# Bias of the values added to the tokens on GpSimd, values evicted as copies, statistics aggregated in groups, and a handicap for VectorE in the planner

## The chip, the cores and the metric

The kernel runs on one core of a Trainium2 chip. The metric is the device time of one execution in microseconds (us). A core has five engines with instruction queues of their own: TensorE (PE in the profile, with PEld for its weight loads), VectorE (DVE), ScalarE (ACT), GpSimd (POOL) and SyncE (SP), which issues most transfers. Each engine works through its queue in the order in which it was written; semaphores hold an instruction back until what it reads is there.

## The reference

Four sequences of 1024 tokens with 256 features go through attention, a channel mix, a state-space block and the channel mix again, each on a normalized copy and added to the token stream `x`:

```python
x = x + _L0_attn_a_ref(_layernorm(x, axis=-1), Wq, bq, Wk, bk, Wv, bv)
x = x + _L0_ffn_ref(_layernorm(x, axis=-1), W_r, W_k, W_v, mu_r, mu_k)
x = x + _L0_attn_b_ref(_layernorm(x, axis=-1), ...)   # state-space block
x = x + _L0_ffn_ref(_layernorm(x, axis=-1), W_r, W_k, W_v, mu_r, mu_k)
```

What the change touches is the attention and the layer norm:

```python
V = jnp.einsum('nsd,ed->nse', X, Wv) + bv
scores = jnp.einsum('nqd,nkd->nqk', Q, K) / scale
scores = jnp.where(causal, -jnp.inf, scores)
weights = jax.nn.softmax(scores, axis=-1)
return jnp.einsum('nqk,nkd->nqd', weights, V)

m = jnp.mean(x, axis=axis, keepdims=True)
v = jnp.var(x, axis=axis, keepdims=True)
return (x - m) / jnp.sqrt(v + eps)
```

The rows of `weights` sum to 1, so `weights @ (V0 + bv)` equals `weights @ V0 + bv`: the bias of the values may be added to `V`, or to what attention adds to.

## The kernel before

**Tiles.** `x[b]` holds the tokens of sequence b on the chip: 128 partitions, 8 row tiles of 256 features. A half `j` (0 to 7) is four row tiles, half a sequence. A row tile `i` runs from 0 to 31. Letters name the stage: `a` attention, `f` the first channel mix, `h` the state-space block, `g` the second channel mix.

**Layer norm.** `normalized` serves all four stages. For each of the four row tiles of a half, `stats(n)` issues bn_stats (L622) and bn_aggr (L623) on VectorE, one behind the other. `ve` adds the epsilon on VectorE (L648, L650), `rs` raises to the power -1/2 on GpSimd (L661), `mrs` makes the shift on VectorE (L670), and `xn` scales and shifts each row tile on VectorE (L676) or ScalarE (L682). In stage g, halves 0 to 5 take their statistics from sums on ScalarE instead. The normalized rows are then turned: through a tile in DRAM and a VectorE transpose (L750), or by TensorE.

**Attention.** `queries` folds the query and key weights into one product. `values(i)` (L1522) multiplies a row tile with `wv`, which has 257 columns: the last is a term that the keys' bias adds to a key's score. VectorE evicts the product into `v` and adds `bv_r` in one instruction (L1532); the 257th column of `bv_r` belongs to that term. `scores(i)` makes the scores (L1550) in a pair of PSUM banks; `least` on VectorE adds the mask (L1560) and, with the 257th column of `v`, takes the least element (L1566); ScalarE exponentiates (L1571). `turn_by_dram` turns the exponentials through DRAM (transpose L1608), `weigh(i)` multiplies them with `v` (L1655), and `a.x` scales and adds that to `x` on VectorE (L1664).

**The rest.** `stream_sums` (T, L832), the gating product `y` (L1965) and `keys_of_batch` feed `seven_products`, which makes four 128x128 block products with seven multiplications (`held_...`, L858); copies between its steps (L783 ScalarE, L784 VectorE) stand on its chain. The channel mixes add to `x` on GpSimd (L1101), the state-space block adds its output bias there too (L1699).

**The planner.** No order is written out by hand. `Order` collects operations with what they need, one or more ways (engine, cost in us, what to emit), and the PSUM bank that they free; matrix products are units. It works out due times backwards and then runs a simulation forwards: at each step `_way` takes the way of an operation that ends first, `_first` the operation with the earliest due time among those that can start about now. `DVE+port` marks VectorE instructions that it doesn't lay beside GpSimd work. Units come from a window of 9, the one that can start soonest. It tries 20 settings with 5 rounds each, keeps the one that ends first by its own clock, and emits the queues in that order. So a changed cost can change the order of every engine in every stage. `PSUM` has 4 single banks and 2 pairs. In the loop over `i`, scores are laid two or three row tiles ahead of `weigh`, values one more.

The lines that the steps below turn on:

```python
        return min(
            (self._start(time, w) + w[1], self._start(time, w), w[0], w[2])
            for w in self.log[n]["ways"]
        )
```

Of the kernel before, what the change touches and what calls it, by code (L numbers as in the profile page):

```python
# [19 lines left out]
P = 128  # L20
NB = 4
L = 1024
D = 256
# [4 lines left out]
NH = NT // 2  # L28
KC = D // P
HALF = 512  # L30
# [23 lines left out]
class Order:  # L54
# [15 lines left out]
    FLIGHT, LANDING = 1.2, 0.24  # L70
    HOLD = 30.0
    SURE = 0.5
    FRONT = 12.0


# [180 lines left out]
    def _way(self, time, n):  # L256

        if self.log[n]["moves"]:
            time = max(time, self.queue - self.FLIGHT - 0.5)
        return min(  # L260
            (self._start(time, w) + w[1], self._start(time, w), w[0], w[2])
            for w in self.log[n]["ways"]
        )

    def _start(self, time, way):
        engine, _, port = way[0].partition("+")
# [93 lines left out]
def dve(n):  # L360
    return 0.02 + n / 850
# [7 lines left out]
def hybrid_kernel(  # L369
# [34 lines left out]
    nc = tc.nc  # L404
# [179 lines left out]
    def normalized(  # L584
# [35 lines left out]

        def stats(n):
            nc.vector.bn_stats(st()[:, n, :], row(n))  # L622
            nc.vector.bn_aggr(mv()[:, n, :], st()[:, n, :])  # L623

        def sums(n):
            nc.scalar.activation(
# [66 lines left out]
        if by_scalar:  # L693
            for n in range(NH):
                o.op(f"{key}.su{n}", [needs[n]], ("ACT", act(D) + 0.11, partial(sums, n)))
            o.op(f"{key}.me", [f"{key}.su{n}" for n in range(NH)], ("POOL", 0.2, means))
            for n in range(NH):
                o.op(f"{key}.st{n}", [f"{key}.me"], ("ACT", act(D) + 0.11, partial(squares, n)))
            variances_of = lambda n0, n1: by_sums()
            shifts_of = lambda n0, n1: shifts_by_sums()  # L700
        else:
            for n in range(NH):
                o.op(f"{key}.st{n}", [needs[n]], ("DVE", 0.53, partial(stats, n)))
            variances_of, shifts_of = variances, shifts
        for n0, n1 in spans:
            span = "" if n1 - n0 == NH else f"{n0}"
            some = range(n0, n1)
            o.op(
                f"{key}.ve{span}", [f"{key}.st{n}" for n in some],
                ("DVE+port", 0.08 * k, partial(variances_of, n0, n1)),  # L710
            )
            o.op(
                f"{key}.rs{span}", [f"{key}.ve{span}"],
                ("POOL", 0.4 + 0.62 * k, partial(powers, n0, n1)),
            )
            o.op(
                f"{key}.mrs{span}", [f"{key}.rs{span}"],
                ("DVE+port", 0.08 * k, partial(shifts_of, n0, n1)),
            )
            for n in some:  # L720
                o.op(
                    f"{key}.xn{n}", [f"{key}.mrs{span}"],
                    ("DVE+port", dve(D), partial(on_vector_by_sums if by_scalar else on_vector, n)),
                    ("ACT", act(D) + 0.1, partial(on_scalar, n)),
                )
# [89 lines left out]
    def stream_sums(key, src, needs):  # L815

        t = [lazy(lambda k=k: cols(f"T{k}_{key}")) for k in range(KC)]

        def b(c, h):
            return src(h)[:, c, :]  # L820

        def sums(k):
            return t[(k - 1) // 2]()[:, (k - 1) % 2, :]

        for k, plus, minus in (
            (1, lambda: b(0, 1), lambda: b(0, 0)),
            (3, lambda: b(1, 1), lambda: b(0, 1)),
            (2, lambda: b(1, 1), lambda: sums(1)),
            (4, lambda: b(1, 0), lambda: sums(2)),
        ):  # L830
            def emit(engine, k=k, plus=plus, minus=minus):
                engine.tensor_sub(sums(k), plus(), minus())  # L832

            o.op(
                f"{key}.T{k}", needs + ([f"{key}.T{k - 1}"] if k in (2, 4) else []),
                ("POOL", 1.05, partial(emit, nc.gpsimd)), ("DVE+port", dve(HALF), partial(emit, nc.vector)),
            )
        return sums

# [597 lines left out]
    def attend_prepare(j, by_hand=False):  # L1437
# [5 lines left out]
            spans=((0, 2), (2, NH)) if j == 0 else ((0, NH),), by_scalar=False,  # L1443
        )

    def attend_transpose(j, spans=((0, NH),)):

        xn, needs, _, _ = xa_rows.pop(j)
# [63 lines left out]
    def values(i):  # L1512
# [7 lines left out]
        def emit():  # L1520
# [8 lines left out]
        )  # L1529
        o.op(  # L1530
            f"v{i}", [f"pv{i}"],
            ("DVE", dve(D), lambda: nc.vector.tensor_add(t()[:, n, :], pv()[:, : D + 1], bv_r)),  # L1532
            frees="bank",
        )

    def scores(i):
# [43 lines left out]
            + ["constants"],  # L1580
            emit, "pair",
        )
        o.op(f"p{i}", [f"sc{i}", f"v{i}"], ("DVE", dve(nk) + 0.3, least), frees="pair")
        o.op(f"e{i}", [f"p{i}"], ("ACT", act(nk) + 0.11, exponents))

    def turn_by_dram(i):
# [60 lines left out]
    def weigh(i):  # L1647
# [23 lines left out]
            [f"pT{k}.{i}" for k in range(t // NH + 1)] + [f"v{NT * b + n}" for n in range(t + 1)],  # L1671
            emit, "bank",
        )
        o.op(f"a.x{i}", [f"po{i}", f"rsm{i}"], ("DVE", dve(D) + 0.05, add), frees="bank")


    xn_rows, xnT, z, py = {}, {}, {}, {}
# [264 lines left out]
    def mix_states(b):  # L1942
# [25 lines left out]
        for h in range(2):  # L1968
            j = 2 * b + h
            for e in range(KC):  # L1970
                o.op(
                    f"g{e}.{j}", [f"pm{b}", f"ss{b}.c{e + 1}{h + 1}"],
                    ("DVE", dve(HALF) + 0.03, partial(grown, j, e)),
                    frees="bank",
                )
                o.op(
                    f"y{e}.{j}", [f"g{e}.{j}", f"z{e}.{j}"],
                    ("POOL", 1.05, partial(gated, nc.gpsimd, j, e)),
                    ("DVE+port", dve(HALF), partial(gated, nc.vector, j, e)),
                )  # L1980

# [283 lines left out]
```

## Time and profile before

| | |
|---|---|
| Median of 3 runs | 465.31 us (464.91 to 465.99) |
| The profiled execution | 464.18 us |
| its span, first to last instruction | 462.4 us |
| Granted TensorE clock | 1.00 |
| Median minus profiled execution | 1.13 us |

The profiled execution is one execution; the 1.8 us outside its span belong to starting and ending it. In the profile a row of instructions reads: line, engine, operation, output <- inputs, shape, count | busy us, mean ns of one | idle time of the engine just before them and what ended it. Some rows that are used later for durations:

```profile
L661 POOL TENSOR_TENSOR rs_h<-ve_h,minus_half 128x8 f32<-128x8 f32 x8 | 13.2, 1646 | 47.9 <-DVE ve_h L650 47.9
L1664 DVE SCALAR_TENSOR_TENSOR x<-po,rsm,x 128x256 f32<-128x256 f32 x32 | 14.9, 467 | 5.4 <-PE po L1655 5.3
L622 DVE BATCH_NORM_STATS2 st_a<-x 128x6 f32<-128x256 f32 x32 | 13.0, 407 | 3.0 <-DMA x<-in_L_attn_a_X_dram 3.0
L977 DVE SCALAR_TENSOR_TENSOR xr_g<-hT_g,mur,xr_g 128x512 f32<-128x512 f32 x16 | 14.4, 920 | 0.5 <-ACT xr_g L974 0.5
```

The stages lie about so in time: attention and the first channel mix, interleaved, up to some 260 us; the state-space block, with the convolution around 302 us, from 260 to some 380 us, its end interleaved with the second channel mix, which goes on to the end.

### The profile page before, as it was taken

What the parts mean: (1) busy time and instruction counts of PE and PEld (TensorE: products, weight loads), DVE (VectorE), ACT (ScalarE), POOL (GpSimd) and SP (SyncE); (2) the same over time, 40 slices, a digit from 0 to 9 for tenths busy, and PEclk for the clock granted to TensorE, in tenths of its full rate; (3) what the DMA queues carried; (4) which work ended last, traced back from release to release, by engine and by line L of the source; (5) the groups of instructions that cost most, each with busy time, mean ns of one, the idle gap of its engine ahead of it and who ended that gap; (6) DMA issues with size and microseconds to landing.
All of it is one profiled execution on the core that took longest, in us unless ns stands there. A gap on an engine that the chain in (4) does not pass through costs nothing.

```text
span 462.4 us, 6630 instructions
## 1 busy us (share of the span) xinstructions
PE 454.6 (98%) x2052; PEld 311.4 (67%) x2052; DVE 370.7 (80%) x914; ACT 227.0 (49%) x473; POOL 139.4 (30%) x145
## 2 busy tenths in 40 slices
PE   8999999999999999999999999999999999999996
PEld 5665776667786767776678774473565857686675
DVE  4898697989989888788989977425689989998852
ACT  3322334453284453554335755523467887743452
POOL 3001002303032412332221568512255216336240
PEclk9999999999999999999999999999999999999999
DMA  8067958684358641428784869503014042604522
GB/s 236 27 170 209 272 143 236 169 252 151 101 160 213 184 138 51 137 87 256 226 261 128 276 220 276 213 15 90 13 63 121 0 143 86 215 14 135 178 75 68
DMA packets 84915, 69.44 MB, mean 150 GB/s; under 512 B 20160, under 2 KB 82576, under 8 KB 84880
## 3 DMA queue, kind: packets, MB, share of 16 engines
q1 hardware_dynamic: 84064, 68.76, 50.2%
q8 instruction: 16, 0.26, 0.2%
q10 hardware_dynamic: 816, 0.26, 0.2%
q14 instruction: 19, 0.16, 0.1%
HBM read 40.54 MB, written 28.45 MB: 149 GB/s over the span
## 4 chain that ended last, share of the span: by engine, by line
PE 84%; DVE 10%; POOL 3%; issue 1%; SPq 1%; DMA 1%; ACT 0%; DVEq 0%; POOLq 0%
PE po L1655 14%; PE sc L1550 13%; PE pv L1522 6%; PE held_zs L858 3%; PE held_ss L858 3%; PE held_qs L858 2%; PE held_gks L858 2%; PE pc L1862 2%; PE dust L1339 1%; DVE T_gks L832 1%; DVE xr_g L977 1%; DVE xk_g L977 1%; POOL x L1101 1%; PE pp_a0.pq L793 1%; PE pp_g6.pk L793 1%
## 5 line engine op out<-in xcount | busy, mean ns | idle before, releaser
L1655 PE MATMUL po<-v,prT 128*128 128x256 f32 x288 | 67.6, 380 | 0.0
L1550 PE MATMUL sc<-xa,q 128*128 128x512 f32 (+3 forms) x192 | 66.9, 486 | 0.0
L1655 PEld LDWEIGHTS po<-v,prT 128*128 128x128 f32 x288 | 54.2, 189 | 11.6 <-issue 3.1
L1571 ACT ACTIVATE pr<-pr,nmx 128x128 f32<-128x128 f32 (+7 forms) x32 | 24.7, 773 | 69.7 <-DVE pr L1566 57.1
L1550 PEld LDWEIGHTS sc<-xa,q 128*128 128x128 f32 x192 | 34.8, 190 | 24.3 <-issue 20.1
L1522 PE MATMUL pv<-wv,xa 128*128 128x257 f32 x128 | 32.7, 380 | 0.0
L1101 POOL TENSOR_TENSOR x<-x,r_f 128x512 f32<-128x512 f32 x16 | 20.8, 1298 | 35.7 <-DVE r_f L1095 33.8
L1522 PEld LDWEIGHTS pv<-wv,xa 128*128 128x128 f32 x128 | 23.9, 191 | 8.4 <-issue 4.1
L1608 DVE STREAM_TRANSPOSE prT<-pblocks 128x384 f32<-128x384 f32 (+7 forms) x30 | 24.0, 798 | 4.8 <-DMA pblocks<-exps 4.8
L661 POOL TENSOR_TENSOR rs_h<-ve_h,minus_half 128x8 f32<-128x8 f32 x8 | 13.2, 1646 | 47.9 <-DVE ve_h L650 47.9
L1566 DVE TENSOR_SCALAR_CACHE_REDUCE pr<-sc,v 128x128 f32<-128x128 f32 (+7 forms) x32 | 26.2, 818 | 1.1
L661 POOL TENSOR_TENSOR rs_a<-ve_a,minus_half 128x4 f32<-128x4 f32 x7 | 7.4, 1060 | 62.8 <-DVE ve_a L648 52.9
L1101 POOL TENSOR_TENSOR x<-x,r_g 128x512 f32<-128x512 f32 x14 | 20.1, 1446 | 16.8 <-DVE r_g L1095 16.8
L1699 POOL TENSOR_TENSOR x<-x,bout_r 128x512 f32<-128x512 f32 x16 | 20.7, 1302 | 13.3 <-ACT x L1692 9.8
L1692 ACT ACTIVATE x<-x,mrs_h,rs 128x256 f32<-128x256 f32 x32 | 17.2, 588 | 6.5 <-DVE rs L1703 6.5
L1965 POOL TENSOR_TENSOR z<-z,skip 128x512 f32<-128x512 f32 x11 | 15.0, 1384 | 17.4 <-DVE skip L1961 17.3
L661 POOL TENSOR_TENSOR rs_f<-ve_f,minus_half 128x4 f32<-128x4 f32 x8 | 8.1, 1016 | 39.2 <-DVE ve_f L648 34.1
L1664 DVE SCALAR_TENSOR_TENSOR x<-po,rsm,x 128x256 f32<-128x256 f32 x32 | 14.9, 467 | 5.4 <-PE po L1655 5.3
L622 DVE BATCH_NORM_STATS2 st_a<-x 128x6 f32<-128x256 f32 x32 | 13.0, 407 | 3.0 <-DMA x<-in_L_attn_a_X_dram 3.0
L974 ACT ACTIVATE xk_g<-hT_g,muk 128x512 f32<-128x512 f32 x16 | 11.0, 713 | 8.4 <-DVE hT_g L750 8.4
L1532 DVE TENSOR_TENSOR v<-pv,bv_r 128x257 f32<-128x257 f32 x32 | 13.2, 413 | 2.2 <-PE pv L1522 1.8
L977 DVE SCALAR_TENSOR_TENSOR xr_g<-hT_g,mur,xr_g 128x512 f32<-128x512 f32 x16 | 14.4, 920 | 0.5 <-ACT xr_g L974 0.5
(478 smaller groups left out, 1070.3 us busy)
## 6 DMA issues: line engine op xcount, KB each, us to landing
hk<-r_dram SPq DMA_DIRECT2D x16, 512.0 KB, 6.6
rows_g<-xn_g SPq DMA_DIRECT2D x8, 512.0 KB, 3.0
blocks_g<-rows_g SPq DMA_DIRECT2D x32, 128.0 KB, 2.7
x<-in_L_attn_a_X_dram SPq DMA_DIRECT2D x7, 512.0 KB, 5.1
rows_f<-xn_f SPq DMA_DIRECT2D x7, 512.0 KB, 3.5
blocks_f<-rows_f SPq DMA_DIRECT2D x28, 128.0 KB, 2.7
rows_h<-xn_h SPq DMA_DIRECT2D x7, 512.0 KB, 3.3
blocks_h<-rows_h SPq DMA_DIRECT2D x28, 128.0 KB, 2.9
```

The source lines that it names most:

```text
L661: nc.gpsimd.tensor_tensor(rs()[:, :k].rearrange("p k n -> p (k n)"), ve()[:, :k].rearrange("p k n -> p (k n)"), minus_half[:, : k * NH], A ...
L858: lambda: nc.tensor.matmul(dst(), lhsT=w(), rhs=data(), start=first, stop=True, skip_group_check=True),
L977: nc.vector.scalar_tensor_tensor(t()[:, c, :], hT()[:, c, :HALF], mu1[:, c : c + 1], t()[:, c, :], ALU.mult, ALU.add,)
L1101: nc.gpsimd.tensor_add(xg, xg, r()[:, ts(g, 2), :])
L1522: nc.tensor.matmul(pv()[:, : D + 1], lhsT=xaj()[:, c, ts(n, P)], rhs=wv[:, c, :], start=(c == 0), stop=(c == KC - 1),)
L1550: nc.tensor.matmul(sc()[:, k * HALF : k * HALF + w], lhsT=qh()[:, c, ts(n, P)], rhs=keys[k]()[:, c, :w], start=(c == 0), stop=(c == KC - 1),)
L1566: nc.vector.tensor_scalar(dst, src, v[2 * b + h]()[:, n, D : D + 1], None, ALU.add, ALU.min, accum_out=nmx(),)
L1571: nc.scalar.activation(p()[:, :nk], p()[:, :nk], AF.Exp, bias=nmx(), scale=-1.0, accum_out=sm())
L1608: nc.vector.transpose(dst()[:, : NH * width].rearrange("p (k m a) -> p k m a", m=NH, a=GRP), blocks().rearrange("p m (k a) -> p k m a", a= ...
L1655: nc.tensor.matmul(po()[:, :D], lhsT=src()[:, ts(n, P)], rhs=v[2 * b + n // NH]()[:, n % NH, :D], start=(n == 0), stop=(n == t),)
L1692: nc.scalar.activation(xt, xt, AF.Identity, bias=mrs()[:, 0, n : n + 1], scale=rs1()[:, n : n + 1])
L1699: nc.gpsimd.tensor_add(xg, xg, bout_r.unsqueeze(1).to_broadcast([P, 2, D]))
```

## The change

It has four parts.

1. The product of the values is evicted as a plain copy of 257 columns, on ScalarE or VectorE. An operation `vc` on GpSimd adds the 257th column of `bv_r` to the 257th column of `v`, and `p` (L1566) needs `vc` instead of `v`. The other 256 columns of the bias are added to the tokens themselves: two operations `b` of each half add `bv_r` to two row tiles of `x` on GpSimd, once their `xn` are made, and `a.x` needs them.
2. `stats` issues bn_stats alone; a new operation `ag` issues the aggregates of a span (four row tiles; two and two in half 0) one behind the other, and `ve` needs it.
3. `_way` adds 0.5 us (`SPARED`) to the end of a VectorE way when it compares the ways of an operation that has more than one. The time it books is the real cost as before.
4. The planner's cost of a GpSimd T (L832) and of a gating product (L1965) is 1.25 us instead of 1.05; that of bn_stats 0.36 us, formerly 0.53 with its aggregate; that of `ag` 0.06 + 0.1 a row.

```diff
+    SPARED = 0.5
...
-        return min(
-            (self._start(time, w) + w[1], self._start(time, w), w[0], w[2])
-            for w in self.log[n]["ways"]
-        )
+        ways = self.log[n]["ways"]
+        best = math.inf
+        for engine, cost, emit in ways:
+            start = self._start(time, (engine, cost, emit))
+            late = start + cost
+            if len(ways) > 1 and engine[:3] == "DVE":
+                late += self.SPARED
+            if late < best:
+                best, chosen = late, (start + cost, start, engine, emit)
+        return chosen
...
         def stats(n):
             nc.vector.bn_stats(st()[:, n, :], row(n))
-            nc.vector.bn_aggr(mv()[:, n, :], st()[:, n, :])
+
+        def gather(n0, n1):
+            for n in range(n0, n1):
+                nc.vector.bn_aggr(mv()[:, n, :], st()[:, n, :])
...
-                o.op(f"{key}.st{n}", [needs[n]], ("DVE", 0.53, partial(stats, n)))
+                o.op(f"{key}.st{n}", [needs[n]], ("DVE", 0.36, partial(stats, n)))
...
+            made = [f"{key}.st{n}" for n in some]
+            if not by_scalar:
+                o.op(
+                    f"{key}.ag{span}", made,
+                    ("DVE", 0.06 + 0.1 * (n1 - n0), partial(gather, n0, n1)),
+                )
+                made = [f"{key}.ag{span}"]
...
-                ("POOL", 1.05, partial(emit, nc.gpsimd)), ("DVE+port", dve(HALF), partial(emit, nc.vector)),
+                ("POOL", 1.25, partial(emit, nc.gpsimd)), ("DVE+port", dve(HALF), partial(emit, nc.vector)),
...
+        def shifted(g):
+            xg = x[b][:, h * NH + 2 * g : h * NH + 2 * g + 2, :]
+            nc.gpsimd.tensor_add(xg, xg, bv_r[:, :D].unsqueeze(1).to_broadcast([P, 2, D]))
+
+        for g in range(2):
+            o.op(
+                f"a{j}.b{g}", [f"a{j}.xn{2 * g + n}" for n in range(2)] + ["wv"],
+                ("POOL", 1.27, partial(shifted, g)), delay=1.0 + g,
+            )
...
-            ("DVE", dve(D), lambda: nc.vector.tensor_add(t()[:, n, :], pv()[:, : D + 1], bv_r)),
-            frees="bank",
+            *copies(lambda: t()[:, n, :], lambda: pv()[:, : D + 1], D + 1), frees="bank",
+        )
+        o.op(
+            f"vc{i}", [f"v{i}"],
+            ("POOL", 0.15, lambda: nc.gpsimd.tensor_add(
+                t()[:, n, D:], t()[:, n, D:], bv_r[:, D:])),
...
-        o.op(f"p{i}", [f"sc{i}", f"v{i}"], ("DVE", dve(nk) + 0.3, least), frees="pair")
+        o.op(f"p{i}", [f"sc{i}", f"vc{i}"], ("DVE", dve(nk) + 0.3, least), frees="pair")
...
-        o.op(f"a.x{i}", [f"po{i}", f"rsm{i}"], ("DVE", dve(D) + 0.05, add), frees="bank")
+        o.op(f"a.x{i}", [f"po{i}", f"rsm{i}", f"a{i // NH}.b{i % NH // 2}"], ("DVE", dve(D) + 0.05, add), frees="bank")
...
-                    ("POOL", 1.05, partial(gated, nc.gpsimd, j, e)),
+                    ("POOL", 1.25, partial(gated, nc.gpsimd, j, e)),
```

More of the change, by code (lines that the diff above doesn't have):

```diff
@@ L707, in normalized @@
             some = range(n0, n1)
+            made = [f"{key}.st{n}" for n in some]
[5 more added lines that the diff above has]
+                made = [f"{key}.ag{span}"]
             o.op(
-                f"{key}.ve{span}", [f"{key}.st{n}" for n in some],
+                f"{key}.ve{span}", made,
                 ("DVE+port", 0.08 * k, partial(variances_of, n0, n1)),
```

## The prediction

> **What bounds the kernel now.** I read the page's busy line first, then the waits of TensorE alone, then the busy times by stretch.
>
> ```profile
> PE 454.6 (98%) x2052; PEld 311.4 (67%) x2052; DVE 370.7 (80%) x914; ACT 227.0 (49%) x473; POOL 139.4 (30%) x145
> ```
> ```profile
> PE dust L1339 <- DVE idle L446: 1.2, 1, 1.2
> PE pr_g4.pv L928 <- ACT ka_g L1047: 0.9, 1, 0.9
> PE held_gks L858 <- DVE u_gks L784: 0.9, 1, 0.9
> PE held_zs L858 <- DVE z L907: 0.6, 1, 0.6
> PE pt_h7.T L775 <- DVE xn_h L676: 0.3, 1, 0.3
> ```
> ```profile
> 24.00:70.00 46.00, 46.00 (x173) 31.84 (x172) 38.74 (x121) 14.87 (x31) 3.70 (x5) 1.00 0.71 198
> ...
> 220.00:260.00 40.00, 40.00 (x165) 30.34 (x164) 35.63 (x89) 18.52 (x34) 10.79 (x11) 1.00 0.68 203
> ...
> 380.00:420.00 40.00, 40.00 (x171) 30.85 (x171) 39.08 (x71) 24.76 (x49) 19.44 (x15) 1.00 0.31 100
> 420.00:432.00 12.00, 10.22 (x34) 5.88 (x33) 8.91 (x22) 6.08 (x11) 3.52 (x5) 1.00 0.49 152
> ```
> The columns are the stretch, its length, then PE, PEld, DVE, ACT, POOL busy, granted clock, DMA share, GB/s. TensorE is idle for 462.4 - 454.6 = 7.8 us: 1.2 before its first matmul, 3.8 behind its last one (432 to 462.4 has 26.62 busy of 30.40, and no wait in between), and four waits of 0.9, 0.9, 0.6 and 0.3 us. Busy is not always full rate, so I also looked at start-to-start times: a 128x512 pass starts 0.43 us after the one before it and a 128x256 pass 0.22 us, nearly everywhere; only the first pass behind a wait takes some 0.1 us more (a pair of 128x512 passes took 1.10 us behind the wait at 425.12, 1.02 at 428.75). The granted clock is 1.00 throughout. The change takes no matmul away and shortens none. So all it can win is 0.9 + 0.9 + 0.6 + 0.3 = 2.7 us and four restarts of 0.1: 3.1 us, 0.7%. From 24 to 260 us, where nearly all of its edited instructions run, TensorE never waits: there it can only lose.
>
> **The values.** `v` leaves VectorE's add (L1532) for a copy on either engine.
>
> ```profile
> L1532 DVE TENSOR_TENSOR v<-pv,bv_r 128x257 f32<-128x257 f32 x32 | 13.2, 413 | 2.2 <-PE pv L1522 1.8
> L1699 POOL TENSOR_TENSOR x<-x,bout_r 128x512 f32<-128x512 f32 x16 | 20.7, 1302 | 13.3 <-ACT x L1692 9.8 <-DMA bout_r<-in_L_attn_b_b_out_dram 3.3
> ```
> One add is busy for 413 ns, but the next instruction starts 0.31 to 0.33 us after it, so VectorE is rid of 32 x 0.33 = 10.6 us if ScalarE takes all of them. ScalarE's 128x256 copy out of PSUM took 0.372 us (the prT copy of L783): 32 x 0.37 = 11.9 us, and it is busy for 104 of the 236 us between 24 and 260 (44%). Cover: TensorE's unbroken work; worth nothing on the path. Uncovered it would give 0.33 us a row.
>
> **The bias on GpSimd.** 16 adds of a 128x512 pair of token tiles are the form of L1699, 1.30 us: 16 x 1.30 = 20.8 us, each with rows that `a.x` (L1664) needs only some steps later. The one-column adds `vc` do not appear in the trace: below lies a memset of 128x2 (0.10 us), above the power of 128x4 (1.02 us). I take 0.23 us, the TENSOR_SCALAR of 128x4 (L631), the nearest shape; 32 of them cost 7 us, between 3 and 33. GpSimd's 53 us between 24 and 260 (23%) become 81 (34%); still idle mostly. But `p` (L1566) on VectorE now waits for `vc` on GpSimd instead of for `v`; behind `p` on VectorE stand the statistics, the transposes and `a.x`, which free the banks that TensorE takes. A late `vc` is covered by the two or three score steps that are laid ahead; without that cover it costs its lateness, up to 1.3 us behind one pair add.
>
> GpSimd's work also holds VectorE up:
>
> ```profile
> 286.04 1.29 POOL L1699 TENSOR_TENSOR x<-x,bout_r 128x512 f32<-128x512 f32 x1
> 286.10 1.31 DVE L670 SCALAR_TENSOR_TENSOR mrs_h<-rs_h,mv_h 128x4 f32<-128x4 f32 x2 [1.15 <-POOL rs_h L661]
> ```
> Two shift instructions, 0.15 us each elsewhere, took 1.31 us because a GpSimd add started 0.06 us ahead. Over the run I count this excess from the means against the undisturbed 0.74 us of L977 (920, 808, 805, 770 ns, 16 each: 5.5 us), the 18 `xn_f` (558 against 405 ns: 2.8 us) and the 16 `mrs_h` (286 against 150: 2.2 us): 10.5 us for 139 us of GpSimd work, 0.075 us for one. The new 28 us bring 2.1 us of it, from zero (if only the planner's gaps are used) to 16 x 1.15 = 18 us (if every add catches one). Net of the 10.6 us this is still a relief.
>
> The Trainium skill says more strictly, on the page "SBUF — State Buffer", section "Who interferes with whom", that GpSimd and a VectorE instruction with two SBUF inputs or in a two-port mode share one exclusive port pair, and that the second to start fully blocks. The row above agrees in kind; by the rule alone every add that meets such an instruction would cost its remainder, by the rows 0.075 us for each us is what met. The rule speaks against moving work from PSUM-fed VectorE instructions, which it calls free of this, to GpSimd adds.
>
> **The statistics.** They go from four pairs to four rows and then four aggregates.
>
> ```profile
> 59.76 0.42 DVE L622 BATCH_NORM_STATS2 st_a<-x 128x6 f32<-128x256 f32 x1
> 60.21 0.18 DVE L623 BATCH_NORM_AGGREGATE mv_a<-st_a 128x2 f32<-128x6 f32 x1
> 60.31 0.39 DVE L622 BATCH_NORM_STATS2 st_f<-x 128x6 f32<-128x256 f32 x1
> 60.74 0.18 DVE L623 BATCH_NORM_AGGREGATE mv_f<-st_f 128x2 f32<-128x6 f32 x1
> ```
> The starts say it: an aggregate waits 0.43 to 0.45 us for its row, what follows it starts 0.10 us later; a pair costs 0.53, four 2.12. Rows followed by something independent are not shown; other 128x256 VectorE instructions follow each other by 0.33 us (two xn_a in 0.73). So four cost 3 x 0.33 + 0.45 + 4 x 0.10 = 1.84 us, at worst 4 x 0.45 + 4 x 0.18 = 2.52. I take 1.84, the rows being independent: 0.28 us less for each of 26 halves, 7.3 us, hidden like the rest. Against it, `ve` comes later behind a last pair of rows: 1.06 us becomes 0.33 + 0.45 + 0.40 = 1.18. This shows only where TensorE waits for a half, `pt_h7` at 288 us: +0.12 us.
>
> **The planner.** VectorE's way of an instruction with two ways is handicapped by 0.5 us, and a GpSimd product costs 1.25 instead of 1.05 (traced: 1.27 to 1.45). Up to 47 `xn` in attention move to ScalarE (47 x 0.59 = 28 us, 44% becomes 61% with the copies), hidden. The stage that could gain is the last, where VectorE is busy for 39.08 of 40 us:
>
> ```profile
> 422.76 1.27 POOL L1101 TENSOR_TENSOR x<-x,r_g 128x512 f32<-128x512 f32 x1
> 422.82 1.23 DVE L670 SCALAR_TENSOR_TENSOR mrs_g<-rs_g,mv_g 128x4 f32<-128x4 f32 x1 [0.54 <-POOL rs_g L661]
> ...
> 424.29 0.68 DVE L784 COPY u_gks<-held_gks 128x512 f32<-128x512 f32 x1
> ```
> The copy of `held_gks` was ready soon after its pass of 420.56, but was given to VectorE, behind `mrs_g` (held 1.23 us) and one `xn_g`; TensorE waited 0.86 us for it. It has a ScalarE way (0.583 us), and ScalarE was free at 423.61. A handicap of 0.5 us is just what turns such a choice: I count this wait with its restart as gone, -0.96. The wait at 325.75 hangs on VectorE behind two skips, a gating product and `z` L907; the one at 431.12 on ScalarE's own relu and square (0.60 + 0.63 us) behind a late pass. Both depend on the new order; I take half of each with its restart: -0.35 and -0.5. Given back: 0.12 at 288 us, and 0.2 for one small wait in attention. What is late next, once the copy is early, is that relu and square of 431.12.
>
> **The sum.** -0.96 - 0.35 - 0.5 + 0.12 + 0.2 = -1.5 us. The profiled execution took 464.18 us, 462.4 of span and 1.8 around it; it becomes 462.7. The median of the runs shown, 465.31, lies 1.13 above it: **463.8 us**.
>
> **Rivals.**
> The waits only move (chance 0.17). Every plan is new, the planner picks by its own clock, and the same 2.7 us stand elsewhere: 465.3. For it: the wait at 431.12 is a chain of latencies that no handicap shortens. Against: the copy at 424.29 is a plain choice of engine.
>
> GpSimd's one-column adds hold up `p` (0.20). Place: GpSimd's queue from 30 to 230 us, with pair adds and powers (1.0 to 1.65 us) ahead of `vc`, and VectorE's queue behind `p`. Price: a wait like the 0.86 us seen. It decides from two such waits on, which eat the gain; with four (one a batch) 463.8 + 4 x 0.86 = 467.2. For it: the 3.70 us of GpSimd work between 24 and 70 us roughly treble (two pair adds for each of some three halves, ten columns), and TensorE's row shows no slack. Against: GpSimd at 34%, and values run a step ahead of scores.
>
> The handicap sends sums and gates to GpSimd (0.13). T (L832) there takes 1.27 instead of 0.68 us and stretches each chain of seven products: six chains between 300 and 430 us x 0.59 = 3.5 us, 463.8 + 3.5 = 467.3. Against: the planner's new 1.25 pulls the other way, 0.62 + 0.5 still being the smaller.
>
> My forecast, faster, has 0.50; its own range is 462.3 (all 3.1 us gone) to 464.3.
>
> **How the numbers follow.** 0.2%, 0.93 us, is about what a measurement of this kernel can tell from no change. Faster 0.50, same 0.17, slower 0.33. The range reaches from 462.3 to 467.6, past the slower cases' values and leaving out their tails, where `vc` costs a power's time or every add catches a VectorE instruction.
>
> **What would show it.** Right: VectorE's busy sum down by 15 us or more, its `v` rows on ScalarE, no TensorE wait between 24 and 260 us, and the wait for `u_gks` gone. `vc` near 0.23 us and rows of statistics starting 0.33 us apart confirm the prices. Wrong: a TensorE wait for `po`, `sc` or `pv` before 260 us, `p` waiting for GpSimd, or more than 2 us of waits between 300 and 432.

## The result: slower by 1.1%

The changed kernel took 469.4 us in the median of 6 runs (469.2 to 471.42), the kernel before 465.35 beside it: a ratio of 1.0108 [1.0092, 1.0125] for the runs compared (the two medians alone stand 0.9% apart). The profiled execution took 469.33 us with a span of 467.5; before, the span was 462.4. The forecast, 463.8 us, had the wrong direction, and the measured time lies above its range.

The work that the change names went as it says. The busy line of the profile after:

```profile
PE 456.9 (98%) x2052; PEld 312.7 (67%) x2052; DVE 338.1 (72%) x826; ACT 262.1 (56%) x558; POOL 169.9 (36%) x196
```

VectorE lost 32.6 us of its 370.7; ScalarE gained 35.1 and GpSimd 30.5. TensorE has the same 2052 passes and 2.4 us more of busy time: some of its passes took longer. The waits of TensorE alone, after (microseconds in total, times, longest):

```profile
PE pr_g5.pr L945 <- DVE xr_g L994: 2.4, 2, 2.1
PE dust L1356 <- DVE idle L453: 1.2, 1, 1.2
PE pt_a0.xa L1482 <- ACT xn_a L692: 1.0, 1, 1.0
PE pr_g4.pv L945 <- ACT ka_g L1064: 0.9, 1, 0.9
PE held_gks L875 <- ACT u_gks L800: 0.7, 1, 0.7
```

Of the four waits of before, three are gone: `u_gks` at 425 us, whose copy went to ScalarE, `z` at 325 and `xn_h` at 288. The fourth, `ka_g`, stands as it was. New are `xn_a` at the start, a `u_gks` of another place (392.6 us) and the large one, `xr_g`; two of 0.2 us are left out here. By stretches of time, after (the columns are those of the prediction's third fence):

```profile
24.00:260.00 236.00, 236.00 (x974) 166.75 (x973) 182.22 (x515) 119.28 (x243) 79.22 (x98) 1.00 0.65 180
...
380.00:420.00 40.00, 39.01 (x163) 29.49 (x162) 37.58 (x63) 26.26 (x59) 11.74 (x11) 1.00 0.29 92
420.00:432.00 12.00, 9.62 (x26) 5.32 (x25) 8.40 (x18) 4.69 (x9) 7.86 (x7) 0.86 0.42 134
```

From 24 to 260 us, where most of the edited instructions run, TensorE is busy without a break, as before. Between 420 and 432 it stands 2.4 us, and the granted clock of that stretch is 0.86.

Where the 5.1 us went, by the start times of the same passes in both traces:

| Stretch (us of before) | lost | by |
|---|---|---|
| up to 24 | +0.7 | both `xn_a` of the first transposition on ScalarE, one behind the other (1.09 us), so a wait of 1.0; 0.18 of it by a bias add |
| 24 to 387 | -1.3 | the waits at 288 and 325 are gone |
| 387 to 420 | +2.4 | waits of 0.7 and 0.16 in a chain of seven products, and eight `py` passes over 2.38 us instead of 1.14 |
| 420 to the end | +3.3 | 1.5 of wait net (2.15 + 0.24 where 0.86 stood), and 1.8 of passes at half rate behind it |

A part of the first loss comes from an edited instruction itself. In the timeline (start, length, engine, instruction; in brackets the wait before it):

```profile
8.62 1.27 POOL L1465 TENSOR_TENSOR x<-x,bv_r 128x512 f32<-128x512 f32 x1
9.26 0.65 DVE L680 SCALAR_TENSOR_TENSOR mrs_a<-rs_a,mv_a 128x2 f32<-128x2 f32 x1
9.94 1.09 ACT L692 ACTIVATE xn_a<-x,mrs_a,rs_a 128x256 f32<-128x256 f32 x2 [0.18 <-DVE mrs_a L680]
```

The first of the new bias adds runs on GpSimd, and VectorE's shift `mrs_a`, which both `xn_a` need, takes 0.65 us beside it; before, without such an add, it took 0.15. ScalarE stands 0.18 us for it, and TensorE for ScalarE. This lies ahead of the 24 us from which the prediction looked for the cost of the adds.

The last stretch, after:

```profile
414.39 1.27 DVE L767 STREAM_TRANSPOSE hT_g<-blocks_g 128x512 f32<-128x512 f32 x2
...
422.16 1.58 POOL L1118 TENSOR_TENSOR x<-x,r_g 128x512 f32<-128x512 f32 x1
422.54 1.22 DVE L680 SCALAR_TENSOR_TENSOR mrs_g<-rs_g,mv_g 128x4 f32<-128x4 f32 x1
423.75 3.04 POOL L1118 TENSOR_TENSOR x<-x,r_g 128x512 f32<-128x512 f32 x2
425.61 1.73 DVE L994 SCALAR_TENSOR_TENSOR xr_g<-hT_g,mur,xr_g 128x512 f32<-128x512 f32 x1
427.39 2.71 PE L945 MATMUL pr_g5.pr<-w_r,xr_g 128*128 128x256 f32 x6 [2.15 <-DVE xr_g L994]
429.90 1.61 PE L875 MATMUL held_gks<-T_gks,fk_sums 128*128 128x512 f32 x2
```

Three GpSimd adds run side by side with VectorE's shift `mrs_g` and its `xr_g`. The shift, a 128x4 instruction, takes 1.22 us, the `xr_g` 1.73 instead of 0.74, and TensorE's six passes wait for it. (The shift alone was held as long before, by the prediction's line of 422.82 us; new is that `xr_g` stands behind it and is held too.) Then these six and two 128x512 passes take 3.95 us to the next start at 431.34, where at full rate (0.22 and 0.43 us each) it would be 2.2: 1.8 us, more than the 1.5 that the waits of this stretch added.

The rows that this `xr_g`, of half 5, is made from were late already. The transfer that writes them to DRAM, before and after:

```profile
399.04 0.38 SPq L738 DMA_DIRECT2D rows_g<-xn_g  x1
```
```profile
406.01 0.38 SPq L755 DMA_DIRECT2D rows_g<-xn_g  x1
```

Seven microseconds later: in the new plan ScalarE, which takes the statistics of this half by its sums, had been given 25 of the 32 `xn_g` rows (before 15) and began its last square of half 5 at 395.5 us instead of 384.8. That took away the slack, but it does not make the wait by itself: ScalarE's part of both `xr_g` was done at 417.7 us,

```profile
416.35 1.32 ACT L991 ACTIVATE xr_g<-hT_g,mur 128x512 f32<-128x512 f32 x2
```

and VectorE, with other work ahead in its queue, came to its own part at 423.69 and 425.61.

### The profile page after: what moved, and what is told of

It is laid out like the page before. It is cut to its first block, busy times and chain, and to the rows that moved or that the text cites. A ratio compares the mean times of both kernels' runs of the same rounds, so it can differ in the third digit from the quotient of the medians.

```text
span 467.5 us, 6710 instructions
## 1 busy us (share of the span) xinstructions
PE 456.9 (98%) x2052; PEld 312.7 (67%) x2052; DVE 338.1 (72%) x826; ACT 262.1 (56%) x558; POOL 169.9 (36%) x196
## 4 chain that ended last, share of the span: by engine, by line
PE 90%; DVE 8%; issue 1%; ACT 1%; DVEq 0%
PE po L1686 13%; PE sc L1581 13%; PE pv L1549 6%; PE held_zs L875 4%; PE held_ss L875 3%; PE held_qs L875 2%; PE held_gks L875 2%; PE pc L1893 2%; DVE T_gks L849 1%; DVE r_g L1112 1%; PE dust L1356 1%; PE pr_g5.pr L945 1%; DVE xk_g L994 1%; DVE xr_g L994 1%; PE py L1982 1%
## 5 line engine op out<-in xcount | busy, mean ns | idle before, releaser
L1563 POOL TENSOR_TENSOR v<-v,bv_r 128x1 f32<-128x1 f32 x32 | 7.5, 235 | 69.1 <-ACT v L800 62.5
L1465 POOL TENSOR_TENSOR x<-x,bv_r 128x512 f32<-128x512 f32 x16 | 20.1, 1268 | 4.1 <-ACT xn_a L692 4.1
L1996 POOL TENSOR_TENSOR z<-z,skip 128x512 f32<-128x512 f32 x10 | 13.5, 1358 | 18.9 <-DVE skip L1992 18.7
L692 ACT ACTIVATE xn_f<-x,mrs_f,rs_f 128x256 f32<-128x256 f32 x22 | 11.9, 594 | 14.9 <-DVE mrs_f L680 14.9
L800 ACT COPY v<-pv 128x257 f32<-128x257 f32 x28 | 10.3, 368 | 16.6 <-PE pv L1549 16.5
L1591 DVE TENSOR_TENSOR sc<-sc,mask 128x128 f32<-128x128 f32 x32 | 9.3, 291 | 12.8 <-PE sc L1581 12.6
L692 ACT ACTIVATE xn_a<-x,mrs_a,rs_a 128x256 f32<-128x256 f32 x27 | 14.6, 590 | 5.6 <-DVE mrs_a L680 5.6
```

The costliest lines, as they stand in the source:

```text
L692: nc.scalar.activation(place(n), split(row(n)), AF.Identity, bias=mrs()[:, k - 1, n : n + 1], scale=rs()[:, k - 1, n : n + 1],)
L1465: nc.gpsimd.tensor_add(xg, xg, bv_r[:, :D].unsqueeze(1).to_broadcast([P, 2, D]))
```

## The experiments

Four theories stood against each other, and the expectations name them by these letters. **A**: the handicap of VectorE fills ScalarE and so costs in the last stage. **B**: the work of the values and their bias (GpSimd's adds) costs. **C**: no part costs in itself; each edit of a planner's cost draws a new order of all engines, and the planner's own clock doesn't see what TensorE will wait for. **D**: the new price of GpSimd's products costs. The medians, and ratios to the kernel before on the same chip (its median was 465.35 us beside the change and 464.4 to 464.8 beside the others, so single times of the change and of the others compare by ratio; the ratio is not always that of the medians):

| Run | what it is | us (lowest to highest) | ratio, interval |
|---|---|---|---|
| e1_no_handicap | change, no handicap | 468.85 (468.0-469.5) | 1.009 [1.0065, 1.0115] |
| e2_handicap_alone | before + handicap | 469.82 (469.54-471.72) | 1.0121 [1.0091, 1.015] |
| e3_handicap_not_g | change, handicap not in stage g | 465.45 (464.88-466.64) | 1.0021 [1.0008, 1.0034] |
| e4_filler | change + 18 idle passes | 468.18 (467.65-470.03) | 1.0084 [1.0054, 1.0114] |
| e5_values_alone | before + values and bias | 463.85 (463.42-464.4) | 0.9978 [0.9966, 0.999] |
| e6_stats_alone | before + statistics | 465.16 (464.03-466.06) | 1.0009 [0.9995, 1.0023] |
| e7_price_alone | before + price of products | 464.79 (464.57-465.74) | 0.9998 [0.9982, 1.0014] |
| e8_control_lag | before, LAG 0.16 | 462.95 (462.84-463.8) | 0.9969 [0.9958, 0.998] |
| e9_after_lag | change, LAG 0.16 | 465.0 (464.84-466.63) | 1.0006 [0.9993, 1.0019] |
| e10_handicap_lag | e2, LAG 0.16 | 465.07 (464.33-465.85) | 1.0005 [0.9994, 1.0017] |
| e11_no_handicap_lag | e1, LAG 0.16 | 467.6 (466.43-468.57) | 1.0055 [1.0036, 1.0073] |
| e12_values_lag | e5, LAG 0.16 | 463.54 (463.49-463.82) | 0.9967 [0.9953, 0.9981] |
| e13_xr_up | change, one instruction moved | 468.56 (466.73-471.45) | 1.0079 [1.0056, 1.0102] |
| e14_no_adds | change, three adds left out | 467.64 (465.53-469.65) | 1.0061 [1.0039, 1.0084] |
| e15_after_lag14 | change, LAG 0.14 | 465.27 (464.61-468.03) | 1.0023 [0.9999, 1.0048] |
| e16_no_handicap_lag14 | e1, LAG 0.14 | 470.73 (469.7-471.57) | 1.0116 [1.0071, 1.0162] |
| e17_control_lag14 | before, LAG 0.14 | 471.02 (470.68-471.37) | 1.0133 [1.0118, 1.0148] |
| e18_values_stats | before + values + statistics | 472.99 (472.79-473.21) | 1.0177 [1.016, 1.0194] |

`LAG` is the time that the planner adds, by its own clock, between the end of an instruction and the start of one that needs it. It changes no instruction's work; it changes only the plan.

### The handicap: taken away, alone, and kept out of the last stage

```diff
-    SPARED = 0.5
+    SPARED = 0.0
```


> The changed kernel with the handicap of VectorE set from 0.5 to 0 us; everything else of the change stays. Theory A (the handicap moves rows of the second channel mix's layer norm to ScalarE, which there also makes the statistics of halves 0 to 5; half 5 comes 7 us late, TensorE waits 2.4 us for its xr and its clock then falls): those waits and the fall of the clock go, 464 to 466 us. Rival B (the GpSimd adds and the copies of the values cost it): still 468 to 470. Rival C (any new plan of this planner lands somewhere): anything from 463 to 470, with waits in other places.

The kernel before with the handicap in `_way` and nothing else:

```diff
+            if len(ways) > 1 and engine[:3] == "DVE":
+                late += self.SPARED
```


> The kernel before with the handicap of 0.5 us alone. Theory A: 468 to 470, with more than 20 of the 32 xn_g rows on ScalarE, half 5 written late and a wait for pr_g5 or its neighbours of over 1.5 us. Rival B: 465 as before. Rival C: anything, with the waits elsewhere.

The change, with the handicap in all stages but g:

```diff
-            if len(ways) > 1 and engine[:3] == "DVE":
+            if len(ways) > 1 and engine[:3] == "DVE" and self.log[n]["key"][0] != "g":
```


> The changed kernel with the handicap in all stages but the second channel mix (operations whose key begins with g). Theory A: 464 to 466, the same gain as without any handicap in the last stage, and the wait at 325 us still gone. Rival B: 468 to 470. Rival C: anything from 463 to 470.

The three do not agree on a culprit. Without the handicap the change stays slow (1.009); the handicap alone is slow too (1.0121); and without it in stage g the change comes down to 1.0021. If the handicap were the cost, the first would have been fast; if it were not, the second would. Their main waits stand at different places, `skip` for 1.9 us in the first and two waits for `ka_g` of 2.3 in all in the second. The second has 20 `xn_g` rows on ScalarE, but no wait for `pr_g5`, which A expected there.

### Each other part alone, and a change of the plan with nothing in it

The kernel before with part 1 of the change alone, with part 2 alone, with the price alone (both 1.05 to 1.25), and with nothing but

```diff
-    LAG = 0.15
+    LAG = 0.16
```


> The kernel before with the first part of the change alone: values as copies, their bias added to the tokens and to one column on GpSimd. Theory C (no part costs by its own work; a new order of the last stage does, because its plan is right only by the planner's own clock): TensorE without waits from 24 to 260 us, and a time from 464 to 470 that hangs on the waits between 380 and 432 us. Rival B (this work costs): over 467, with waits before 260 us or a late vc behind them. Theory A (handicap only): 464 to 466.

> The kernel before with the statistics grouped, alone. It changes nothing of halves 0 to 5 of the second channel mix, whose statistics ScalarE makes. Theory A: 464 to 466. Theory C: 464 to 470, hanging on the waits between 380 and 432 us, which the grouped statistics have no instruction in before 412 us.

> The kernel before with GpSimd's price of sums and gating products at 1.25 us, alone; no instruction is added or removed. Theory D (the price moves sums and gates to VectorE, the fuller engine of the last stage): over 467, with more of T_gks and of the gating products on VectorE than before. Theory A: 464 to 466. Theory C: 464 to 470.

> A control: the kernel before, with the planner's allowance from the end of one instruction to the start of what waits for it at 0.16 us in place of 0.15. Not one instruction differs in kind or number; only the order and the engine of two-way work are new. Theory C: this too is slower, 466 to 470, by waits of TensorE between 380 and 432 us, though nothing of the change is in it. Theories A, B and D: 464 to 466, as before.

No part alone is slower: the values gain 0.2%, the statistics and the price can't be told from no change. In these plans B does not hold for the values alone, nor D for the price alone. The control is the fastest kernel of the study, 462.95 us, and has nothing of the change in it; C had expected it slower, at 466 to 470, and the other theories at 464 to 466. Its waits of TensorE:

```profile
PE dust L1339 <- DVE idle L446: 1.2, 1, 1.2
PE pr_g4.pv L928 <- ACT ka_g L1047: 0.9, 1, 0.9
PE held_gks L858 <- DVE ka_g L905: 0.7, 1, 0.7
```

So one hundredth of a microsecond in a planning constant moves the time by 0.3%, more for the better than the best single part. This kernel beats both that are compared.

### The same programs, drawn again

The change, the handicap alone, the change without handicap and the values alone, each with LAG 0.16 in place of 0.15:

> The changed kernel whole, with the planner's allowance at 0.16 us: the same instructions, another plan. Theory A (the handicap in the last stage costs, whatever the plan): 467.5 to 471, with over 20 xn_g rows on ScalarE and waits of 3 us or more between 380 and 445 us. Theory C (each plan is a draw, and the change drew a bad one): the draws seen without the handicap run from 463.0 to 468.9, most of them 463 to 465.5; so it lies there with no tie to the handicap.

> The kernel before with the handicap alone and the allowance at 0.16 us. Theory A: 467.5 to 471 again. Theory C: 463 to 465.5 most likely.

> The changed kernel without the handicap (468.9 with the allowance at 0.15), with the allowance at 0.16 us. If the other three parts together cost 4 us by their work: 467.5 to 470 again. If the first draw was bad (one wait of 1.9 us and the clock behind it): 463 to 466.

> The kernel before with the values' part alone and the allowance at 0.16 us, each of which was faster alone (463.9 and 463.0). If the two gains have their own causes: 462.0 to 463.2. If each is a good draw: 463 to 465.5.

A falls here: with the handicap in every stage the change takes 465.0 and the handicap alone 465.07, within 0.1% of the kernel before beside them. The rows of half 5, at 406.0 us in the first plan of the change, are written at 400.8 in its second, and the wait for `xr_g` is not there:

```profile
400.77 0.38 SPq L755 DMA_DIRECT2D rows_g<-xn_g  x1
```

In the second plan of the handicap alone they are written at 406.1, as late as in the change, and no pass of `pr_g5` waits: VectorE makes the two `xr_g` at 419.1 and 421.0 us. So the late rows alone are not the cause; the place of `xr_g` in VectorE's queue counts.

The change without the handicap came out at 467.6, not at the 463 to 466 of a better draw: the expectation of C failed there.

B falls a second time for the values alone: with this LAG they leave TensorE the same waits as the control with it, to the tenth, but for one of 0.2 us at the start that only the control has, and their ratios to the kernel before are 0.9967 and 0.9969. In the two traces, control and then values, the stretch from 24 to 260 us:

```profile
24.00:260.00 236.00, 236.00 (x974) 166.59 (x973) 205.42 (x567) 102.81 (x197) 55.16 (x57) 1.00 0.64 178
```
```profile
24.00:260.00 236.00, 236.00 (x974) 166.74 (x973) 199.70 (x552) 110.01 (x216) 77.39 (x96) 1.00 0.65 179
```

GpSimd works 22 us more, VectorE 6 less, and TensorE is busy throughout in both.

### What makes the wait and its tail

The first filled TensorE's idle time ahead of the late pass with passes that nothing reads; the second issued the second shift product `xr1` of half 5 right behind `xr0` in VectorE's queue, the plan being the same; the third left three of the GpSimd adds out, so that six row tiles of the output lack their last term.

```diff
+    if key == "g5.pr0" and j == 0 and c == 1:
+        for _ in range(18):
+            nc.tensor.matmul(pr()[:, 1, :], lhsT=idle[:, :P], rhs=idle[:, :D], start=True, stop=True, skip_group_check=True)
```


> The changed kernel, same plan, with 18 matmuls of nothing (bf16, 128x256, some 0.11 us each, 1.9 us together) in TensorE's queue just where it waits 2.15 us for the second half of xr_g of half 5; they write a place that is overwritten later. If the slower matmuls behind that wait (0.427 us a pass in place of 0.216 for some 4 us) come from the idle time, the granted clock between 420 and 432 us is 1.00 and the time is 467.3 to 467.8 (1.6 to 2.1 us less, the wait itself stays). If the clock falls for another reason, 469.2 to 469.6 or more.

```diff
-        if self.emits:
+        if self.emits and e["key"] != "g5.xr1":
             emit()
+            if e["key"] == "g5.xr0":
+                self.log[self.made["g5.xr1"]]["ways"][0][2]()
```


> The changed kernel with its plan, except that VectorE's xr_g of half 5, second column (425.61 us in the trace after), is issued right behind the first (423.69 us) instead of behind one block sum and two rows of statistics. If VectorE's order there makes the loss: TensorE's wait for xr_g falls from 2.15 to some 0.8 us, the clock between 420 and 432 us stays at 1.00, and the time is 466 us (1.3 us of wait and 2.0 us of slow passes less). If the loss has other causes: 469.2 to 469.6.

```diff
-        if self.emits:
+        if self.emits and e["key"] not in ("g2.x0", "g2.x1", "g3.x0"):
```


> The changed kernel with its plan, leaving out three GpSimd adds of the second channel mix (x of half 2, both pairs, and the first pair of half 3), so six row tiles of the output lack the last term. If GpSimd's hold on VectorE (mrs_g 1.22 us and xr_g 1.73 us there, 0.15 and 0.74 us elsewhere) makes VectorE late: mrs_g and xr_g take 0.15 and 0.74 us, the wait falls under 0.8 us, the clock stays, 465.5 to 466.2 us. If VectorE's order alone does: the wait stays over 1.5 us.

The filler, by stretch and in the timeline:

```profile
420.00:432.00 12.00, 11.56 (x50) 7.39 (x50) 9.90 (x21) 4.97 (x10) 7.88 (x7) 1.00 0.40 130
```
```profile
425.33 2.13 PE L947 MATMUL pr_g5.pr<-idle 128*128 128x256 bf16 x18
427.65 1.56 PE L951 MATMUL pr_g5.pr<-w_r,xr_g 128*128 128x256 f32 x6 [0.19 <-DVE xr_g L1000]
```

`xr_g` is no earlier, but the six passes behind it take 1.56 us instead of 2.71 and the clock of the stretch is 1.00 instead of 0.86. So the tail comes from the idleness of TensorE and not from anything that the passes read. The other executions agree: three of the four with the filler show a mean clock of 0.998 or more, all six of the change 0.996 or less. The span of the profiled execution is 466.1 us against the change's 467.5; the ratio, 1.0084 [1.0054, 1.0114], overlaps with the change's, so the saving is seen in the profile and not told apart by the times; the median, 468.18, lies above the 467.3 to 467.8 expected.

Without the adds:

```profile
423.17 0.14 DVE L680 SCALAR_TENSOR_TENSOR mrs_g<-rs_g,mv_g 128x4 f32<-128x4 f32 x1
...
425.17 0.72 DVE L994 SCALAR_TENSOR_TENSOR xr_g<-hT_g,mur,xr_g 128x512 f32<-128x512 f32 x1
425.94 1.56 PE L945 MATMUL pr_g5.pr<-w_r,xr_g 128*128 128x256 f32 x6 [0.55 <-DVE xr_g L994]
```

The shift takes 0.14 us where it took 1.22, `xr_g` 0.72 where it took 1.73, the wait 0.55 where it was 2.15, and the six passes run at full rate. The adds make 1.6 us of the wait: that is shown. These two rows agree with the Trainium skill, page "SBUF — State Buffer", section "Who interferes with whom", by which a VectorE instruction with two SBUF inputs contends with a GpSimd instruction that reads SBUF for a shared pair of ports. With `xr1` moved up the wait was 1.2 us in two pieces, the largest 0.9, and no pass of that stretch ran at half rate, though `xr_g` was still held:

```profile
PE pr_g5.pr L947 <- DVE xr_g L996: 1.2, 2, 0.9
```
```profile
428.73 2.42 DVE L996 SCALAR_TENSOR_TENSOR xr_g<-hT_g,mur,xr_g 128x512 f32<-128x512 f32 x2
428.79 3.49 POOL L1120 TENSOR_TENSOR x<-x,r_g 128x512 f32<-128x512 f32 x2
```

So VectorE's order and GpSimd's adds make the wait together. In time, the run without the adds gains (1.0061 [1.0039, 1.0084], below the change's interval); with `xr1` moved up the intervals overlap. Neither came near what was expected: medians of 467.64 and 468.56 against 465.5 to 466.2 and 466. Executions of one program lay 4 to 5 us apart here, and eight of ten of each show a mean clock of 0.996 or less; where it fell in those that were not profiled is not recorded. In the profiled one with `xr1` moved up the clock fell at 13 us instead, behind the wait for `xn_a` of 1.2 us, in the slowest of its ten executions: eight 128x512 passes took 6.08 us to the next start, where behind a like wait of 1.17 us in the filler's profile they took 3.54. Between 380 and 420 us its clock was 0.96 besides. I had counted on one place of trouble; with it mended, the others of the same plan remain.

### More draws, with and without the handicap

> The changed kernel whole, allowance 0.14 us: a third plan of it. Theory C: 463 to 469, most likely 464 to 466; whatever it is, more than 467 only with a wait of TensorE over 1.8 us and a fall of the clock behind it. If the change costs by its work: 467 or more without such a wait.

> The changed kernel without the handicap, allowance 0.14 us: a third plan of it. Theory C: 463 to 469, most likely 464 to 466. If values, statistics and price together cost by their work: 467 to 469 a third time.

> A second control: the kernel before, allowance 0.14 us. If a plan of any of these programs is a draw from one urn (463 to 471): over 467 is as likely as not. If the kernel before draws from a better one than the combined parts: 463 to 465.5 for the third time, without a TensorE wait over 1.5 us.

> Values and statistics together, with the old price of 1.05 us and no handicap. If the price of 1.25 us, by which sums and gates go to VectorE, is what the slow three share: 463 to 465.5. If values and statistics together are enough: 467 to 470.

The first is the change with LAG 0.14, the second the same without handicap, the third the kernel before with LAG 0.14 and nothing else, the fourth the kernel before with parts 1 and 2. The third shows that what theory C names is enough: with no edit of the change in it, the kernel before takes 471.02 us, slower than the change. Its waits and its stretch from 300 to 315 us:

```profile
PE held_ss L858 <- DVE u_ss L784: 4.5, 1, 4.5
```
```profile
300.00:315.00 15.00, 10.52 (x70) 5.16 (x66) 5.44 (x7) 4.32 (x8) 3.83 (x3) 0.81 0.01 3
```
```profile
307.38 0.75 DVE L907 SCALAR_TENSOR_TENSOR z<-held_zs,b_all,u_zs 128x512 f32<-128x512 f32 x1 [5.42 <-ACT z L1755]
308.04 1.74 DVE L832 TENSOR_TENSOR T_zs<-xnT,T_zs 128x512 f32<-128x512 f32 x1
309.71 0.41 DVE L1829 COPY bp<-pbt 128x256 f32<-128x256 f32 x1
310.04 0.68 DVE L784 COPY u_ss<-held_ss 128x512 f32<-128x512 f32 x1
```

The head of VectorE's queue waited 5.42 us for a ScalarE instruction, and the copy that TensorE needed stood three places behind it. By kernel, the draws, in us above or below the kernel before (LAG 0.15) on the same chip:

| | LAG 0.14 | 0.15 | 0.16 | mean |
|---|---|---|---|---|
| before | +6.2 | 0 | -1.7 | +1.5 |
| the whole change | +0.7 | +4.1 | +0.2 | +1.7 |
| the change without handicap | +6.1 | +4.5 | +2.8 | +4.5 |
| handicap alone | - | +5.4 | +0.3 | +2.9 |
| values alone | - | -0.8 | -1.2 | -1.0 |

Three draws of the same kernel before lie 7.9 us apart; the whole change is 0.2 above it in the mean of three, which is nothing against that. The one pattern left is that values and statistics together, without the handicap, drew four slow plans of four (467.6 to 473.0; two of them, 470.7 and 473.0, above every range expected). Of the nine plans that lack one of the two parts or both, two were slow (471.0 and 469.8); of the four with both and the handicap, in all stages or all but g, one. In the slowest the same place fails as in the change, harder:

```profile
425.30 4.01 DVE L679 TENSOR_SCALAR xn_g<-x,mv_g,rs_g 128x256 f32<-128x256 f32 x3
425.35 3.80 POOL L1111 TENSOR_TENSOR x<-x,r_g 128x512 f32<-128x512 f32 x3
...
431.94 3.78 PE L938 MATMUL pr_g5.pr<-w_r,xr_g 128*128 128x256 f32 x8 [3.60 <-DVE xr_g L987]
```

Three rows that should take 1.2 us take 4.0 beside three GpSimd adds. The wait doesn't need the handicap. Whether these two parts lead to worse plans as a rule, or four draws were unlucky, stays open, and with it whether the handicap mends what they cost.

## Why the prediction was wrong

**The step that failed is the sum's three planner terms, "-0.96 - 0.35 - 0.5"**, with the sentence that all it can win is 3.1 us and that between 24 and 260 us it can only lose. I took the new order to be the old one with waits removed. The profile after has a new order in every stage. The old waits went even better than I had them: `u_gks` gone (-0.96 predicted), `z` at 325 wholly gone (half), `xn_h` gone (+0.12 predicted); only `ka_g` stayed (half). What the sum lacked were the new ones: +0.7 at the start, +2.4 between 387 and 420 and +3.3 from 420 on. The 0.2 given back for one small wait in attention had no row behind it; the wait came at the first transposition, as the 0.7. The text said that the planner picks by its own clock and gave this as a rival, "the waits only move", at 465.3; the rival had the right mechanism and the wrong price, since it let the same 2.7 us stand elsewhere. The kernel before drawn again shows what a new plan may bring: from -1.7 to +6.2 us. Of the signs listed, those for being right came, all of them (the wait for `u_gks` at 425 us is gone, though one of 0.7 stands at 392.6), and so did one for being wrong: 3.25 us of waits between 300 and 432 (0.70, 0.16, 0.24 and 2.15).

**The second failure is the bound.** "The granted clock is 1.00 throughout" was read as a property of the kernel; it was a property of a plan whose longest wait, before the first matmul, is 1.2 us and whose others are under 1. Behind the 2.15 us wait came 1.8 us of half-rate passes, where I had 0.1 for a restart. So no slower case reached 469. (The lower bound, by the text's own 3.1 us, would be 462.2 and not 462.3; nothing hangs on it.)

**The prices were right.** The one-column adds, the pair adds and the copies, after:

```profile
L1563 POOL TENSOR_TENSOR v<-v,bv_r 128x1 f32<-128x1 f32 x32 | 7.5, 235 | 69.1 <-ACT v L800 62.5
L1465 POOL TENSOR_TENSOR x<-x,bv_r 128x512 f32<-128x512 f32 x16 | 20.1, 1268 | 4.1 <-ACT xn_a L692 4.1
L800 ACT COPY v<-pv 128x257 f32<-128x257 f32 x28 | 10.3, 368 | 16.6 <-PE pv L1549 16.5
```

235 ns against 0.23 us, 1268 against 1.30, 368 against 0.372; 28 of the 32 copies went to ScalarE. The statistics:

```profile
413.13 1.07 DVE L629 BATCH_NORM_STATS2 st_g<-x 128x6 f32<-128x256 f32 x3
414.12 0.36 DVE L633 BATCH_NORM_AGGREGATE mv_g<-st_g 128x2 f32<-128x6 f32 x4
414.39 1.27 DVE L767 STREAM_TRANSPOSE hT_g<-blocks_g 128x512 f32<-128x512 f32 x2
```

Rows start 0.33 us apart and four aggregates are done in 0.27, so four rows cost 4 x 0.33 + 0.27 = 1.59 us, less than my 1.84. That all of this is hidden was right as well: no wait of TensorE between 24 and 260 us, and the rival of GpSimd's one-column adds, 467.2, is refuted by that row and by the two runs of the values alone. `p` did wait for the one-column add, once, for 0.3 us, behind TensorE's work.

**The hold of GpSimd** I priced at 0.075 us for each us of its work, as a load on VectorE hidden like the rest. As a load that may be; where it met VectorE's `mrs_g` and `xr_g` with TensorE waiting, it made 1.6 us of wait, as the run without the adds shows. The prediction's own fences showed two shifts of 0.15 us each stretched to 1.31 at 286 us and one to 1.23 at 422.82; I used that for a mean over the run and not for the stage where nothing covers it.

**The rival of sums and gates on GpSimd** hardly happened in the change: GpSimd has 13 of the 32 sums T where it had 10 (of `T_gks` 2 of 12 where it had 3) and 10 of the 16 gating products where it had 11; the dearer price pulled back as argued. With the handicap alone, at the old price, all 32 and all 16 went there in both plans; they took 469.82 and 465.07 us, so their place doesn't decide alone.

**What its slowness is, then.** The 1.1% belongs to this plan: with other lags the same change stands 0.2 and 0.7 us above the kernel before, and the kernel before with one stands 6.2 above itself. A cost or a gain of the parts that three draws each, spread over 4 to 8 us, can't show stays open; for values and statistics without the handicap the four slow draws speak for a cost.

## What to carry to other kernels

Where a planner lays out the order of all engines, an edit of any cost is a new draw: before a change is credited or blamed, draw the old kernel again with a constant moved by a hair, and compare families of plans and not two plans. Price the worst of a new plan by such draws, and not by the waits that the old plan happens to have. In a stage that TensorE barely fills, look for each VectorE instruction on its path that may run beside a GpSimd add, since the planner's separation of the two holds only by its own clock.

## What the runs showed of the hardware

A wait of TensorE can cost nearly double its length. In the profiled executions, waits of 1.6, 1.7 and 1.8 us (e3, e9, e6) were followed by passes at full rate; waits of 1.9 us (e1), 2.0 (e2), 2.15 (the change), 2.5 (e11), 3.6 (e18) and 4.5 (e17) by some 4 us of passes at half rate, a 128x256 pass in 0.43 us instead of 0.22. Two passes of the same form behind the waits of e9 and e11:

```profile
327.24 1.12 PE L875 MATMUL held_zs<-T_zs,w_in 128*128 128x512 f32 x2 [1.66 <-DVE z L924]
```
```profile
426.43 2.07 PE L875 MATMUL held_gks<-T_gks,fk_sums 128*128 128x512 f32 x2 [2.48 <-DVE u_gks L801]
```

In e16 the passes right behind a wait of 2.4 us still ran at full rate, and the next eight, behind 0.5 us more, at half:

```profile
429.08 1.10 PE L875 MATMUL held_gks<-T_gks,fk_sums 128*128 128x512 f32 x2 [2.41 <-ACT u_gks L800]
430.69 3.68 PE L945 MATMUL pr_g5.pr<-w_r,xr_g 128*128 128x256 f32 x8 [0.52 <-DVE xr_g L994]
```

These are one execution of each plan, and the runs show no length that divides the two cases: of the executions that were not profiled, one each of e1, e11 and e16 and two of e2 have a mean clock of 1.000, and one of e3 and two of e9 have 0.994 or 0.995. The Trainium skill, page "TensorE: Matmul & The Clock Gate", section "HAM oscillation — how this bites in real kernels", warns of idle gaps above about 3.4 us; here 1.9 to 2.15 us were enough in the profiled executions, and by that rule the change's wait would have cost its length alone. Near the start 1.2 us were enough in one execution (the one with `xr1` moved up) and 1.17 us were not in another (the filler's).

One program's executions differ as such falls would make them: the ten of e15 lie at 464.6 to 465.5 (six, clock 0.998 to 1.0) and 467.3 to 468.0 (four, clock 0.995 to 0.996). And a 128x4 VectorE instruction can be held for 1.22 us by a GpSimd add, nearly nine times its own 0.14.
